# Layer 0's weights loaded in fewer transfers on two queues, and the first stripe's buffers in another place

## Chip, cores and metric

The kernel runs on one core of a Trainium2 chip. The metric is device time in microseconds (us), median over runs. The engines are TensorE (PE; its weight loads are PEld), VectorE (DVE), ScalarE (ACT), GpSimd (POOL) and SyncE (SP). SP issues DMA transfers; in the kernel before, it issues all of them.

## The reference, cut to what matters

The input `x` is (2, 96, 96, 96): two images of 96 channels, 96 x 96. Two layers follow each other, each with a mixer and a feed-forward network, both with residuals.

```
# layer 0
x = x + conv0(ln_c(x), weights)       # see below
t = tokens(x); t = t + ffn0(ln_t(t)); x = back(t)
# layer 1
x = x + conv1(ln_c(x), weights)       # attention on pooled queries, depthwise 5x5
t = tokens(x); t = t + ffn1(ln_t(t)); x = back(t)

# conv0, for each window of 6 x 6 (k: four scan directions, d: 192 channels, n: 16 states)
xin, z = split(in_proj_w @ x); z = silu(z)
t   = gelu(bn(conv3x3(xin, off1_w)))           # offsets: fr = sigmoid(2 * off2_w @ t)
xs  = bilinear(xin, fr)
x_dbl = x_proj @ xs                            # 6 rows for dt, 16 for B, 16 for C
delta = softplus(dt_projs_weight @ x_dbl[:6] + dt_projs_bias)
A   = -exp(A_logs)
h   = h * exp(delta * A) + delta * xs * B      # scan over the 36 tokens
y   = sum_n(h * C) + Ds * xs
out = out_proj @ (ln(y) * z)
```

The weights that this case is about are small: `dt_projs_weight` (4, 192, 6), `dt_projs_bias` (4, 192), `A_logs` (768, 16) and `Ds` (768). One weight is large: `off1_w` (192, 192, 3, 3), 1296 KB.

## The kernel before

`tile_metaformer` makes constants, then calls `_layer0` and `_layer1`. `_layer0` has two parts.

The first part loads and prepares weights. `_l0_weights` (from L265 on) loads, in this order and all from SP: `in_proj`, `off1`, `out_proj`, `ln_g`, `ln_b` (L272), `bn` (L289), `off2` (L301), `x_proj` (L308). Then, for each of four directions `kg`, it loads two pieces of `dt_w` (L323, L324) and six of `dt_b` (L330, L333), each 32 numbers that land one to a partition. DVE rearranges `dt_w` into `w_dt` (L340, L346). `A_logs` is rearranged through a scratch tensor `ad` in DRAM: 16 transfers write it (L381), four read it back into `at0` (L387), DVE rearranges that into `at` (L390), PE transposes it into `pa` (L392), ACT takes the exponential into `k.A` (L395). `Ds` follows (L400). DVE also builds selection matrices from the identity: `selb` (L359, 24 copies), `minus` and `fold`. `_ffn_weights` loads four arrays (L248). All temporaries of this part come from a pool `l0t`, and PSUM from a pool `l0p`; both are closed before the second part.

The second part works on 32 stripes of six image rows. `front(n)` (`_l0_front`) loads the rows of stripe n into `xt` (L464), normalises (first matmul on x: `axc`, L475), projects, convolves (`pc`, L536), samples (`top`, `bot`), and writes `delta` and `delta * x` to DRAM (`dl_d`, `du_d`). `_l0_scan` reads them back, repeated for the 16 states (`dlr`, `dur`, L983; `cre`, L993), and for 64 units a stripe does `dA` on ACT (L997), `bp` on DVE (L1011), the scan `h` on DVE (L1021), `h * C` on POOL (L1024) and the sum on PE (L1034). `back(n)` does the rest and the feed-forward network.

The order in this second part is not that of the code. `_Plan` takes each operation with an estimated cost and a due time, simulates five engines and issues the operations by that; `_in_order` then ties each engine to that order, SP included. The plan starts at zero and knows nothing of the weights. Ahead of the plan, in the weights' part, the layer that builds the program orders each engine's instructions itself. It also gives each transfer one of eight completion semaphores in turn; a transfer that takes a semaphore waits until the transfer that had it last has landed. Memory is handed out as a stack: a pool that opens takes the place of one that has closed, and its first users wait for those who used that place. In the kernel before, `front` is the first pool that opens after `l0t` closes:

```
P.front, P.hand, P.rep, P.back = (pool(n, 1) for n in ("front", "hand", "rep", "back"))
P.ps = pool("ps0", 1, space=PSUM)
```

`_layer1` loads its weights (L1692, L248, `lb` L1706) and then, image by image, stripes `nxt` of the scratch tensor `x2d` that layer 0 wrote (L1108; first matmul `nxc`, L1113).

Of the kernel before, what the change touches and what calls it, by code (L numbers as in the profile page):

```python
# [8 lines left out]
F32 = mybir.dt.float32  # L9
# [16 lines left out]
C = 96  # L26
# [7 lines left out]
NS = 16  # L34
KG = 4
NQ = 4
CB = 32
NBL = C // CB
PAST = 1e33
EXP_LN = 6  # L40
NG = 12
# [14 lines left out]
def _in_order(k, tc, start, engines=ENGINES):  # L56

    last = {}
    for i in k.nc.cur_bb.bb.instructions[start:]:
        if i.engine in engines:  # L60
            if i.engine in last:
                tc.add_manual_dep(
                    i,
                    last[i.engine].name,
                    mybir.DependencyInfo(
                        mybir.DependencyClass.NoSync, mybir.DependencyReason.DATA
                    ),
                    reason="in_order",
                )
            last[i.engine] = i  # L70
# [170 lines left out]
def _ffn_weights(k, const, tmp, pre, W1t, b1t, W2t, b2t):  # L241

    nc = k.nc
    w = Ctx()

    def quantized(src, shape, name, keep8):
        f = tmp.tile(shape, F32, tag=name, name=pre + name)
        nc.sync.dma_start(f, src)  # L248
        q = (const if keep8 else tmp).tile(shape, F8, tag=pre + name + "q", name=pre + name + "q")
        nc.vector.tensor_copy(q, f, saturate=False)  # L250
        if keep8:
            return q
        g = const.tile(shape, F32, tag=pre + name + "g", name=pre + name + "g")
        nc.vector.tensor_copy(g, q)
        return g

    w.w1 = quantized(W1t, [C, HID], "w1", True)
    w.w2 = quantized(W2t, [128, NM, C], "w2", True)
    w.b1 = quantized(b1t, [128, NM], "b1", False)
    w.b2 = quantized(b2t, [C, 1], "b2", False)  # L260
    return w
# [5 lines left out]
def _l0_weights(k, a, cp, tmp, ps, dram):  # L267
    nc = k.nc
# [45 lines left out]
    dt_w = tmp.tile([C, 2, 3, 128], F32, tag="dt_w", name="dt_w")  # L314
# [4 lines left out]
    for kg in range(KG):  # L319
        o, kk = kg % 2, kg // 2  # L320
        nc.vector.tensor_copy(k.w_dl[:, :, o, kk * 6 : kk * 6 + 6], xp[:, :, kg, 0:6])
        rows = slice(kk * 6, kk * 6 + 6)
        nc.sync.dma_start(dt_w[rows, o, kk, :], a["dt_w"][kg, :, 0:128])  # L323
        nc.sync.dma_start(dt_w[rows, o, 2, kk * 64 : kk * 64 + 64], a["dt_w"][kg, :, 128:])  # L324
        b = a["dt_b"]
        for blk in range(2 * NBL):
            half, r = divmod(blk, NBL)
            src = b[r * CB : r * CB + CB, kg, half : half + 1]
            if blk < 4:
                nc.sync.dma_start(k.dt_b[blk::4, o, kk : kk + 1], src)  # L330
            else:
                r0 = kk * 64 + blk - 4
                nc.sync.dma_start(k.dt_b[r0 : kk * 64 + 64 : 2, o, 2:3], src)  # L333
        for j in range(4):
            src = xp[:, :, kg, 6 + NS :] if j == 1 else xp[:, :, kg, 6 : 6 + NS]
            nc.vector.tensor_copy(k.w_bc[:, :, o, j, kk, :], src)

    for o in range(2):
        for m in range(2):
# [4 lines left out]
        for kk in range(2):  # L344
            cols = slice(kk * 64, kk * 64 + 64)
# [31 lines left out]

    ad = dram.tile([NS, KG * 2, C], F32, tag="ad", name="ad")
    src = a["A_logs"].rearrange("(n d) (k g) -> n d k g", n=NS, g=NG)
    for n in range(NS):  # L380
        nc.sync.dma_start(ad[n].rearrange("k (d g) -> d k g", g=NG), src[n])  # L381
    na = KG * 2 * NBL
    at0 = tmp.tile([NQ * na, NQ, CB], F32, tag="at0", name="at0")
    at = tmp.tile([NQ * na, 128], F32, tag="at", name="at")
    rows = ad.rearrange("(q i) k (b c) -> i (k b) q c", i=NQ, c=CB)
    for i in range(NQ):
        nc.sync.dma_start(  # L387
            at0[i * na : (i + 1) * na], rows[i]
        )
    nc.vector.tensor_copy(at.rearrange("p (c q) -> p q c", c=CB), at0)  # L390
# [6 lines left out]


    ds4 = tmp.tile([C, KG, 2], F32, tag="ds4", name="ds4")
    nc.sync.dma_start(ds4, a["Ds"])  # L400
    k.Dsum = cp.tile([C, 2], F32, tag="Dsum", name="Dsum")
    nc.vector.tensor_tensor(k.Dsum, ds4[:, 0], ds4[:, 1], ALU.add)
    nc.vector.tensor_tensor(k.Dsum, k.Dsum, ds4[:, 2], ALU.add)
# [532 lines left out]
def _l0_scan(k, P, S, n, f, tau):  # L936


    nc = k.nc
    f.Y = S.tile(P.hand, [C, 2, T], "Y", 1)  # L940
    for h in range(2):

        py = S.tile(P.ps, [128, 512], "y", 1)
        t0 = (64 * n + 32 * h) * tau

        def direct(h=h, py=py):

            for b in range(NBL):
                w = k.w_D[:, h, b * CB : b * CB + CB]
                v = f.xs0.ap[:, h]  # L950
                nc.tensor.matmul(py.ap[b * CB : b * CB + CB, :HEAD], w, v[:, :HEAD],
                                 start=True, stop=False)
                nc.tensor.matmul(_tail(py, b), w, v[:, HEAD:], start=b == 0, stop=False)

        S.op("pe", 1.4, direct, (f.xs0,), (py,), due=t0)
        for o in range(2):
            for kk in range(2):
                _l0_section(k, P, S, f, o, h, kk, py, t0 + (16 * o + 8 * kk) * tau, tau)

        def out(h=h, py=py):  # L960
            nc.scalar.copy(f.Y.ap[:, h, :HEAD], py.ap[:C, :HEAD])
            for b in range(NBL):
                nc.scalar.copy(f.Y.ap[b * CB : b * CB + CB, h, HEAD:], _tail(py, b))

        S.op("act", 1.4, out, (py,), (f.Y,), due=t0 + 33 * tau)
# [84 lines left out]
def _layer0(k, tc, a, x, x2d):  # L1050


    nc = k.nc
    with ExitStack() as st:
        P = Ctx()
        pool = lambda name, bufs, **kw: st.enter_context(tc.tile_pool(name=name, bufs=bufs, **kw))
        cp = pool("l0c", 1)
        P.dram = pool("scr", 1, space=DRAM)
        with ExitStack() as ws:
            tmp = ws.enter_context(tc.tile_pool(name="l0t", bufs=1))  # L1060
            wps = ws.enter_context(tc.tile_pool(name="l0p", bufs=1, space=PSUM))
            _l0_weights(k, a, cp, tmp, wps, P.dram)
            ffn = _ffn_weights(k, cp, tmp, "f0", a["W1_0"], a["b1_0"], a["W2_0"], a["b2_0"])
        P.front, P.hand, P.rep, P.back = (pool(n, 1) for n in ("front", "hand", "rep", "back"))
        P.ps = pool("ps0", 1, space=PSUM)
        P.early = {"pe": 60, "act": 60, "dve": -30, "pool": 0, "sp": 8}
        P.np, P.ng, P.nda, P.nh = 3, 5, 2, 6
        start = len(nc.cur_bb.bb.instructions)
        S, tau = _Plan(k), 3.4
        stripes = [(b, s) for b in range(NB) for s in range(NW)]  # L1070
        F = [Ctx() for _ in stripes]

        def front(n):
            if n < len(stripes):
                t0, t1 = (64 * n - 90) * tau, (64 * n - 12) * tau
                _l0_front(k, P, S, F[n], x, *stripes[n], lambda v: t0 + v * (t1 - t0))

        def back(n):
            b, s = stripes[n]
            t0, t1 = (64 * n + 68) * tau, (64 * n + 135) * tau  # L1080
            _l0_back(k, P, S, F[n], ffn, x[b, :, s * WIN : (s + 1) * WIN, :],
                     x2d[b, :, s * T : (s + 1) * T], lambda v: t0 + v * (t1 - t0))

        front(0)
        for n in range(len(stripes)):
            front(n + 1)
            _l0_scan(k, P, S, n, F[n], tau)
            back(n)
        S.issue()
        _in_order(k, tc, start, ENGINES + (mybir.EngineType.SP,))  # L1090
# [660 lines left out]
def tile_metaformer(ctx: ExitStack, tc: tile.TileContext, a, out):  # L1751
# [33 lines left out]
    scratch = ctx.enter_context(tc.tile_pool(name="x2d", bufs=1, space=DRAM))  # L1785
    x2d = scratch.tile([NB, C, NTOK], F32, tag="x2d", name="x2d")
    _layer0(k, tc, a, a["x"], x2d)
    _layer1(k, tc, a, x2d, out)

# [61 lines left out]
```

## Time and profile before

| what | us |
|---|---|
| median of 3 runs (lowest, highest) | 9014.57 (9014.46, 9014.84) |
| profiled execution: its own time | 9021.88 |
| profiled execution: span, first to last instruction | 9020.1 |
| SP's first issue | 0.75 |
| issue of the first `xt` | 44.44 |
| first matmul on x (`axc`) | 47.60 |
| first scan (`h`, L1021) | 178.82 |
| last `h * C` of layer 0 on POOL (L1024) starts | 6889.72 |
| first matmul of layer 1's stripes (`nxc`) | 6933.29 |

| engine | busy us | share of the span |
|---|---|---|
| PE | 7473.2 | 83% |
| DVE | 8098.6 | 90% |
| ACT | 6393.2 | 71% |
| POOL | 6194.7 | 69% |

A share is a mean over stages with different limits: layer 0 runs to about 6900 us, layer 1 after it. Rows of the timeline give start, length, engine, line, operation, output and input, and in brackets how long the engine was idle before and what ended it. Rows of the waits give who waited for what, the total, the number of times and the longest. A row of SP (`SPq`) is the issue of a transfer, not its data movement. "xN" is a group of N instructions, merged.

### The profile page before, as it was taken

The numbers are of one execution on the slowest core, as the hardware profiler recorded it, in microseconds if no ns is written. First come the engines' busy times: TensorE is split into PE (matmuls) and PEld (weight loads), VectorE is DVE, ScalarE is ACT, GpSimd is POOL, SyncE is SP. The second block draws the span as 40 slices with busy tenths as digits, with TensorE's granted clock in tenths as the row PEclk, the third lists the DMA queues.
The fourth block names the chain that finished last, engine by engine and source line by source line (L and its number), as shares of the span: only waits on it lengthen the run. The fifth ranks groups of instructions, "written<-read, shape, count | busy, mean of one in ns | idle before, by whom it ended". The sixth has DMA issues, their size and how long they took to land.

```text
span 9020.1 us, 122080 instructions
## 1 busy us (share of the span) xinstructions
PE 7473.2 (83%) x43537; PEld 3552.9 (39%) x43537; DVE 8098.6 (90%) x5663; ACT 6393.2 (71%) x10720; POOL 6194.7 (69%) x3931
## 2 busy tenths in 40 slices
PE   6888788888878887888788888878866999989998
PEld 3343334444434443344344444334423333543345
DVE  2999999999999999999999999999996898969988
ACT  4677777777777777777777777777754777677867
POOL 3988888888888888888888888898874000320013
PEclk9889888988888888888898989888866999999999
DMA  2444444444444444444444444444442000010000
GB/s 75 138 140 142 140 139 145 140 141 141 135 140 139 135 147 140 141 142 139 144 140 137 142 136 141 137 140 139 138 140 68 3 3 4 21 30 2 3 9 24
DMA packets 335679, 969.58 MB, mean 107 GB/s; under 512 B 50424, under 2 KB 52144, under 8 KB 334768
## 3 DMA queue, kind: packets, MB, share of 16 engines
q1 hardware_dynamic: 335056, 961.64, 33.7%
q8 instruction: 346, 5.67, 0.3%
q14 instruction: 277, 2.27, 0.1%
HBM read 788.04 MB, written 132.17 MB: 102 GB/s over the span
## 4 chain that ended last, share of the span: by engine, by line
DVE 39%; PE 14%; issue 3%; ACT 2%; POOL 1%; DVEq 1%; DMA 0%; SPq 0%; POOLq 0%; ACTq 0%
DVE h L1021 19%; DVE bp L1011 11%; DVE sums L1426 6%; PE sc L1352 4%; DVE acc L1585 3%; PE av L1413 3%; PE y L1034 1%; PE pp L1601 1%; PE pd L669 0%; PE nxc L1113 0%; POOL e L1550 0%; DVEq L1021 0%; PE pk L1125 0%; PE px L608 0%; PE pv L1157 0%
## 5 line engine op out<-in xcount | busy, mean ns | idle before, releaser
L1024 POOL TENSOR_TENSOR h<-h,cre 128x864 f32<-128x864 f32 x2048 | 4122.8, 2021 | 826.7 <-DVE h L1021 415.0
L1021 DVE TENSOR_TENSOR_SCAN h<-dA,bp 128x864 f32<-128x864 f32 x2048 | 4001.5, 1954 | 252.3 <-PE y L1034 6.4
L997 ACT ACTIVATE dA<-dlr,A 128x576 f32<-128x576 f32 x3072 | 2157.0, 765 | 1219.5 <-DVE h L1021 1127.9
L1011 DVE TENSOR_TENSOR bp<-dur,B 128x864 f32<-128x864 f32 x2048 | 2175.8, 1062 | 257.2 <-DMA dur<-du_d 45.5
L1034 PE MATMUL y<-h,fold 128*32 128x288 f32 (+2 forms) x18432 | 1877.9, 454 | 106.3 <-POOL h L1024 102.2
L1008 PE MATMUL B<-bt,selb 128*128 128x288 bf16 x2048 | 637.6, 313 | 1095.3 <-DVE bp L1011 1087.5
L536 PE MATMUL pc<-xin,off 96*96 96x288 f32 x4608 | 1325.0, 414 | 0.9 <-ACT xin L501 0.9
L1034 PEld LDWEIGHTS y<-h,fold 128*32 128x32 f32 x18432 | 766.0, 119 | 1359.0 <-issue 623.2
L1356 ACT ACTIVATE pr<-sc 128x960 f32<-128x960 f32 (+1 forms) x1080 | 955.4, 937 | 258.0 <-DVE sums L1426 146.1
L1426 DVE TENSOR_TENSOR sums<-sums,pr 128x1920 f32<-128x1920 f32 (+1 forms) x510 | 1059.2, 2077 | 60.2 <-ACT pr L1356 7.0
L536 PEld LDWEIGHTS pc<-xin,off 96*96 96x96 f32 x4608 | 708.0, 164 | 622.8 <-issue 379.9
L1507 POOL MEMSET vch<- 96x32 f32 x16 | 2.0, 125 | 1312.8 <-DVE dist L1385 1269.0
L1352 PE MATMUL sc<-qH,kH 32*128 32x480 f32 (+1 forms) x3240 | 710.2, 602 | 9.8 <-DMA q<-qH 9.8
L1352 PE MATMUL sc<-q,kH 32*128 32x480 f32 (+1 forms) x1080 | 564.3, 602 | 0.0
L1413 PE MATMUL av<-pr,vT 128*32 128x480 f32 (+1 forms) x4320 | 532.9, 564 | 3.8 <-ACT av L1430 3.5
L1585 DVE SCALAR_TENSOR_TENSOR acc<-vch,lepe_w,acc 96x1152 f32<-96x1152 f32 x304 | 489.9, 1612 | 7.6
L1008 PEld LDWEIGHTS <-selb 128*128 128x128 bf16 x2048 | 201.9, 100 | 710.5 <-issue 634.5
L1352 PEld LDWEIGHTS sc<-qH,kH 32*128 32x128 f32 x3240 | 285.0, 184 | 439.6 <-issue 304.3
L709 PE MATMUL pt<-xd,w_dt 96*128 96x288 f32 x768 | 317.5, 506 | 25.9 <-ACT zs L519 13.9
L728 POOL TENSOR_TENSOR e<-e,du 128x576 f32<-128x576 f32 x192 | 271.0, 1412 | 32.2 <-ACT du L724 32.0
L1550 POOL TENSOR_TENSOR e<-e,mask 100x384 f32<-100x384 f32 x96 | 171.5, 1808 | 175.6 <-ACT e L1548 175.3
L730 POOL TENSOR_TENSOR dl<-dl,r 128x576 f32<-128x576 f32 x192 | 270.2, 1407 | 6.2
(260 smaller groups left out, 10182.2 us busy)
## 6 DMA issues: line engine op xcount, KB each, us to landing
cre<-c_d SPq DMA_DIRECT2D x1024, 288.0 KB
dur<-du_d SPq DMA_DIRECT2D x256, 864.0 KB
dlr<-dl_d SPq DMA_DIRECT2D x256, 864.0 KB
x<-xs SPq DMA_DIRECT2D x512, 72.0 KB
du_d<-du SPq DMA_DIRECT2D x128, 288.0 KB
dl_d<-dl SPq DMA_DIRECT2D x128, 288.0 KB
du_d<-du SPq DMA_DIRECT2D x128, 144.0 KB
dl_d<-dl SPq DMA_DIRECT2D x128, 144.0 KB
```

Of the source, the lines that this page charges most:

```text
L536: pe(H2, lambda: nc.tensor.matmul(pc.ap[:C, :H2], k.w_c1[:, ih, tap, oh * C : (oh + 1) * C], xin.ap[:, ih, 3 * c + dy : 3 * c + dy + 3, dx ...
L997: S.op("act", 0.76, lambda blk=blk: nc.scalar.activation(dA.ap[:, :, blk, :], dlr.ap[:, blk, :].rearrange("p (c n) -> p c n", c=2), AF.Exp ...
L1008: S.op("pe", 0.3, lambda: nc.tensor.matmul(pB.ap[:, :H2], k.selb[:, kk, i, :], f.bc[o].ap[:, toks], start=True, stop=True), (f.bc[o],), (p ...
L1011: S.op("dve", 1.13, lambda: nc.vector.tensor_tensor(bp.ap[:, : NBL * H2].rearrange("p (b n) -> p b n", b=NBL), dur.ap[:, :, toks], pB.ap[: ...
L1021: nc.vector.tensor_tensor_scan(hv, dv, bv, 0.0, ALU.mult, ALU.add)
L1024: S.op("pool", 2.06, lambda: nc.gpsimd.tensor_tensor(ht.ap, ht.ap, cre.ap[:, toks].unsqueeze(1).to_broadcast([128, NBL, H2]), ALU.mult), ( ...
L1034: nc.tensor.matmul(dst, k.fold, v, start=False, stop=stop)
L1352: nc.tensor.matmul(two[s // 2][:, s % 2, :n], kH[rows, k0 : k0 + 128], q, start=True, stop=True)
L1356: nc.scalar.activation(pr[:, 2 * i : 2 * i + 2, :n], two[i][:, :, :n], AF.Exp, scale=HD**-0.5)
L1413: nc.tensor.matmul((main if s < HEADS else other)[s * HD : (s + 1) * HD, :n], vT[:, blk, hd, :], pr[:, s, :n], start=at == 0, stop=at == e ...
L1426: nc.vector.tensor_tensor(sums[:, :, :n], sums[:, :, :n], pr[:, :, :n], ALU.add)
L1585: S.op("dve", 1.6, lambda: nc.vector.scalar_tensor_tensor(acc.ap, src(), W.lw[:, t : t + 1], acc.ap, ALU.mult, ALU.add), (vch,), (acc,))
```

## The change

Transfers of `dt_w`, `ad`, `at0` and `Ds` are issued by ACT instead of SP. The 24 pieces of `dt_b` become one load of `b`, and PE puts the numbers in their places with four small matmuls: `take` and `take2` are columns of the identity in the right order. The 16 transfers into `ad` become eight, cut along another axis. In PSUM, a tile `beside` of three banks is taken and never used, ahead of `pb`. In `_layer0`, `rep` is the first pool to open after `l0t` closes, and `front` the last. In the kernel after, lines below this place in the file are 14 higher.

```
@@ _l0_weights
-        nc.sync.dma_start(dt_w[rows, o, kk, :], a["dt_w"][kg, :, 0:128])
-        nc.sync.dma_start(dt_w[rows, o, 2, kk * 64 : kk * 64 + 64], a["dt_w"][kg, :, 128:])
-        b = a["dt_b"]
-        for blk in range(2 * NBL):
-            half, r = divmod(blk, NBL)
-            src = b[r * CB : r * CB + CB, kg, half : half + 1]
-            if blk < 4:
-                nc.sync.dma_start(k.dt_b[blk::4, o, kk : kk + 1], src)
-            else:
-                r0 = kk * 64 + blk - 4
-                nc.sync.dma_start(k.dt_b[r0 : kk * 64 + 64 : 2, o, 2:3], src)
+        nc.scalar.dma_start(dt_w[rows, o, kk, :], a["dt_w"][kg, :, 0:128])
+        nc.scalar.dma_start(dt_w[rows, o, 2, kk * 64 : kk * 64 + 64], a["dt_w"][kg, :, 128:])
...
+    b = tmp.tile([C, KG, 2], F32, tag="b", name="b")
+    nc.scalar.dma_start(b, a["dt_b"])
+    take = tmp.tile([C, 2, 128], F32, tag="take", name="take")
+    take2 = tmp.tile([C, 64], F32, tag="take2", name="take2")
+    nc.vector.memset(take, 0.0)
+    for blk in range(2 * NBL):
+        half, r = divmod(blk, NBL)
+        cols = k.ident[:C, r * CB : r * CB + CB]
+        nc.vector.tensor_copy(take[:, half, blk::4] if blk < 4 else take2[:, blk - 4 :: 2], cols)
+
+    ps.tile([128, 3, 512], F32, tag="beside", name="beside")
+    pb = ps.tile([128, 2, KG], F32, tag="pb", name="pb")
+    for half in range(2):
+        nc.tensor.matmul(pb[:, 0], take[:, half], b[:, :, half], start=half == 0, stop=half == 1)
+    nc.vector.tensor_copy(
+        k.dt_b[:, :, 0:2].rearrange("p o k -> p k o"), pb[:, 0].rearrange("p (k o) -> p k o", o=2))
+    for kk in range(2):
+        rows = slice(kk * 64, kk * 64 + 64)
+        nc.tensor.matmul(pb[rows, 1, :2], take2, b[:, 2 * kk : 2 * kk + 2, 1], start=True, stop=True)
+    nc.vector.tensor_copy(k.dt_b[:, :, 2], pb[:, 1, :2])
...
-    for n in range(NS):
-        nc.sync.dma_start(ad[n].rearrange("k (d g) -> d k g", g=NG), src[n])
+    dst = ad.rearrange("n k (d g) -> n d k g", g=NG)
+    for d in range(8):
+        nc.scalar.dma_start(dst[:, d], src[:, d])
...
     for i in range(NQ):
-        nc.sync.dma_start(
+        nc.scalar.dma_start(
             at0[i * na : (i + 1) * na], rows[i]
         )
...
-    nc.sync.dma_start(ds4, a["Ds"])
+    nc.scalar.dma_start(ds4, a["Ds"])
@@ _layer0
-        P.front, P.hand, P.rep, P.back = (pool(n, 1) for n in ("front", "hand", "rep", "back"))
+        P.rep, P.hand, P.back, P.front = (pool(n, 1) for n in ("rep", "hand", "back", "front"))
```

## The prediction

> **What bounds the kernel now.** I read the page first: the span and the slices of part 2.
>
> ```profile
> span 9020.1 us, 122080 instructions
> DVE  2999999999999999999999999999996898969988
> ```
>
> After the first slice (225 us each) DVE is busy 90% or more in every slice up to about 6890 us, that is, all through layer 0. There the time is 2048 units of one `bp` product and one scan. Four-fifths of the first slice is no such work, so I read its timeline. First DVE, where the loop begins:
>
> ```profile
> 172.36 1.06 DVE L1011 TENSOR_TENSOR bp<-dur,B 128x864 f32<-128x864 f32 x1 [45.46 <-DMA dur<-du_d]
> 178.82 1.95 DVE L1021 TENSOR_TENSOR_SCAN h<-dA,bp 128x864 f32<-128x864 f32 x1 [5.39 <-ACT dA L997]
> 180.88 1.06 DVE L1011 TENSOR_TENSOR bp<-dur,B 128x864 f32<-128x864 f32 x1
> ```
>
> From 178.82 on DVE has no idle time worth naming (a unit takes 3.23 us: 16 scans from 191.57 to 243.30). Whatever moves this start moves the end. What leads to it is `front(0)`, one chain from the first matmul on x. The waits of PE in the first 60 us (total, times, longest) say what that waits for:
>
> ```profile
> PE pa L392 <- DVE at L390: 42.2, 1, 42.2
> PE axc L475 <- DMA xt<-in_x: 5.0, 1, 5.0
> ```
>
> And the SP queue (start, length) says why `xt` is late:
>
> ```profile
> 1.21 0.41 SPq L272 DMA_DIRECT2D off<-in_off  x1
> ...
> 9.51 0.27 SPq L324 DMA_DIRECT2D dt_w<-in_dt_w  x1
> 9.82 2.49 SPq L330 DMA_DIRECT2D dt_b<-in_dt_b  x4
> ...
> 22.79 0.48 SPq L323 DMA_DIRECT2D dt_w<-in_dt_w  x1
> ...
> 27.37 10.90 SPq L381 DMA_DIRECT2D ad<-in_A_logs  x16
> 38.31 0.46 SPq L400 DMA_DIRECT2D ds<-in_Ds  x1
> 38.88 1.58 SPq L387 DMA_DIRECT2D at<-ad  x4
> ...
> 44.44 0.31 SPq L464 DMA_DIRECT2D xt<-in_x  x1
> ```
>
> The reader is to see 66 issues in a row, mostly 0.3 to 0.7 us each, and the load of x as the 67th. `axc`, the first matmul on x, starts at 47.60, 3.16 us after the issue of `xt`.
>
> [...] 6% DMA share in 27.3 to 38.3 us agrees that the small ones cost issue, not bandwidth; ACT issues none in this trace. [...] 1.52 us from the issue of `dt_w` (22.79) to DVE's copy of it (24.31), and 1.69 for `Ds` (38.31 to 40.00). [...] `off1` has a bar of 0.41 us and was waited for until 9.51.
>
> **The change, part by part.** *Transfers.* 24 `dt_b` pieces become one; 16 of `ad` become 8; `dt_b`, `dt_w`, `ad`, `at0` and `Ds` go to ACT. SP keeps 13 issues ahead of `xt`, ACT gets 22. In the built order each transfer takes one of eight completion semaphores in turn, over both queues, and waits for the one eight before it. So ACT's seventh `dt_w` (L323, kg 3) waits for `off1`. `off1` is still second on SP; the 1024 packets of the old `ad` filled 6% of 11 us, so ACT's few hundred small packets delay it by some 0.1 us: issue at 9.6 instead of SP's 9.51. Its landing at +1.5, and that of the eighth `dt_w` (issue 10.0, +1.3 as 23.31 to 24.62): 11.1 and 11.3.
>
> *DVE.* In the built order all eight `w_dt` copies now stand ahead of the rest of DVE's set-up, so DVE stands still until 11.3, and is past them at 11.6. Queued behind are: `less_mean`, its fellow and `join` 0.39 (2.54 to 2.93); six `take` copies at 0.16 (nearest row `w_bc`, 0.17) 0.95; `join` 0.18; four `selb` at 0.175 (10 in 1.75) 0.70; two copies of `pb` 0.30, with a wait for PE's four new matmuls that the trace doesn't show, between 0 and 1.5, taken as 0.5. Sum 3.0: 14.6. Then the run that went from 10.22 to 14.42 before (`w_outb` to the last `w_bc`): 4.2, 18.8. Then 16 `selb` 2.8, `minus` and `fold` 0.43, `Dsum` 0.16, `f0w1q` 0.36: 22.55. Only now comes the copy `at`.
>
> *PE.* From the start of `at` to the end of ACT's `A` was 1.10 us (41.74 to 42.84), and in the built order `axc` still stands behind `pa` and waits for that `A`. So `axc` starts at about 23.7.
>
> *What is hidden behind this.* ACT after 10.3: six `ad` at 0.63, with short semaphore waits, to 14.2; `Ds` to 14.7; table and square root for `bn_s` 1.6 (10.36 to 11.96), 16.3; four `at0` at 0.4, 17.9; landing 1.28 after the last issue (40.46 to 41.74), 19.2. SP: `bn` waits for the eighth `dt_w` (11.3), then eight issues with waits for ACT's transfers; `xt` waits for `Ds` to land (14.2 + 1.7) and issues at about 16.5; x is there at 16.5 + 3.16 = 19.7. Both are some 3 us ahead of DVE; this cover gone, the start follows them one for one. `bn_s` at 16.3 is there before DVE wants it (about 17). Pool's two clears wait for nothing now. So what is late next is DVE's own set-up, not x.
>
> *Place.* `rep` lies on the weights' temporaries now, `front` does not. The first `cre` load waits for DVE work that is over by then: nothing. From `axc` on, each engine has the same instructions in the same order through layer 0, so 47.60 to 178.82 is kept, and the loop too. Gain here: 47.60 - 23.7 = 23.9.
>
> *The seam to layer 1.* In the built order, three loads `nxt` that SP issued early now stand behind `lb`:
>
> ```profile
> 6892.97 1.25 SPq L1108 DMA_DIRECT2D nxt<-x2d  x3
> ...
> 6930.41 0.42 SPq L1706 DMA_DIRECT2D lb<-in_lepe_b  x1
> ```
>
> The first issues at 6930.9. With 3.0 us for 216 KB (`xt`, 252 KB, 3.16) it is there at 6933.9; PE used it at 6933.29 (behind `lb` and `proj_b`). Loss 0.6, bounds 0 (it lands within 2.4) and 1.5 (the later two queue as well).
>
> Sum: 23.9 - 0.6 = 23.3. The profiled execution, span 9020.1 and own time 9021.88, should come to 8996.8 and 8998.6. It stands 7.3 us above the median of the runs, 9014.57, and none of the steps lies in that difference: 9014.57 - 23.3 = **8991.3**.
>
> **The rivals.** *ACT's queue binds.* The trace has no issue on ACT. If ACT pays twice SP's price, the nine issues after `off1` take 10.2 instead of 5.1: 19.8; `bn_s` 21.4; four `at0` 24.6; landing 25.9; `axc` 27.0; time 8994.6. At three times it is 33.7, and 9001.3. For it: all of `A` hangs on that queue. Against: SP's bars depend on the transfer's shape, nothing in them is SP's own. *x binds* (DVE quicker, or the semaphore waits shorter): `axc` at 19.7, 8987.3. Against: it needs DVE to lose 4 us of counted rows. *The start is swallowed*: some wait in layer 0 or at the seam stands at its place, and the gain is gone, 9014. Against: DVE's waits from 177 to 6893 sum to under 40 us, and none ends on anything but work that moves with the start. *Slower.* The pools' new order moves every buffer of the loop. If a unit of 3.23 us, in the loop of 2048, became 11.4 ns longer, the gain would be gone; above 20.2 ns (0.6%) the kernel is slower by over 0.2%; at 25 ns it gives 9014.57 - 23.3 + 51.2 = 9042.5. For it: all addresses move. Against: the same instruction has the same 1.95 us in buffers at different places (six for `h`, two for `dA`, `dur`). That the change doesn't free x at all would also end at 9014; the built order speaks against it: `xt` is SP's 14th issue, with one wait.
>
> **How the numbers follow.** About 0.2%, 18.0 us, is what a measurement of this kernel tells from no change: the line is 8996.5. DVE's set-up binds: 0.71, own range 8988.5 to 8994.5 (the wait for PE, 0.1 to 1 us for `off1`, the seam). ACT binds: 0.14, at twice the price or less 0.10, beyond the line 0.04. x binds: 0.06. Swallowed, in whole or by a third: 0.06. Slower: 0.03. Faster 0.87, no change 0.10, slower 0.03. The range from 8987.0 to 8997.5 leaves out about 0.12 in all, and takes in the dearer issue on ACT.
>
> **What would show it.** Right: `xt` issued near 16.5; ACT's seventh `dt_w` near 9.6; the copy `at` on DVE near 22.5, with DVE busy, not waiting, before it; `axc` near 23.7; the first scan near 154.9; `nxc` 0 to 1.5 us further behind the last `x2d` store. Wrong: ACT's issue bars above 1 us, or DVE idle before `at` with ACT still issuing (ACT binds); `axc` right behind `xt` (x binds); a unit other than 3.23 us; a gain at the first scan that the end of layer 0 doesn't show.

## The result, and the profile after

Six runs of the changed kernel have a median of 8985.09 us (8979.85 to 8988.45), six of the kernel before 9014.70 (9009.83 to 9028.03): ratio 0.9965, 95% interval [0.9952, 0.9977]. The forecast was 8991.3, with a range from 8987.0 to 8997.5: right in sign and in how the start is shortened, 6.2 us off in size, and 1.9 us outside the range. The same kernel was run again beside the experiments. Over all runs the kernel before has a median of 9015.93 (102 runs, 9006.83 to 9030.68) and the changed one 8988.07 (32 runs, 8979.85 to 9003.71); their means differ by 27.6 ± 2.1 us, where 23.3 was forecast. (A ± stands for 95%, from the spread of the timed runs alone.)

The page of the changed kernel, its span and DVE's slices:

```profile
span 8986.7 us, 122060 instructions
DVE  3999999999999999999999999999996998969988
```

Layer 0 is bounded by DVE as before; only the first slice has changed, from 2 to 3 tenths. What PE waits for in the first 60 us (total, times, longest, in us):

```profile
PE pb L343 <- DVE take L338: 13.2, 1, 13.2
...
PE pa L406 <- DVE Dsum L417: 7.6, 1, 7.6
```

The waits of before, 42.2 us for `at` and 5.0 for `xt`, are gone. PE's long waits are now for DVE: the small matmuls that spread `dt_b` until 13.20, and then `pa`. (`pa` reads `at`; the wait is put down to `Dsum`, the DVE row that ends at the same time.) The PE timeline (start, length, instruction, idle time before it and what ended it):

```profile
22.44 0.39 PE L406 MATMUL pa<-ident,at 96*128 96x96 f32 x1 [7.59 <-DVE Dsum L417]
23.23 2.85 PE L489 MATMUL axc<-xt,less_mean 96*96 96x384 f32 x4 [0.39 <-ACT A L409]
```

`axc`, the first matmul on x, starts at 23.23 instead of 47.60, and its releaser is ACT's `A`; x itself had landed at 20.54, by the records of landings in the trace. DVE's timeline says why `at` is late:

```profile
9.94 0.28 DVE L353 COPY w_dt<-dt_w 96x128 f32<-96x128 f32 x1 [7.05 <-DMA dt_w<-in_dt_w]
...
11.91 0.20 DVE L359 COPY w_dt<-dt_w 96x64 f32<-96x64 f32 x1 [0.31 <-DMA dt_w<-in_dt_w]
...
14.25 0.16 DVE L344 COPY dt_b<-pb 128x4 f32<-128x4 f32 x1 [0.66 <-PE pb L343]
...
18.73 2.60 DVE L372 CAST selb<-ident 32x128 bf16<-32x128 f32 x16
...
22.02 0.27 DVE L404 COPY at<-at 96x128 f32<-96x128 f32 x1
156.16 1.95 DVE L1035 TENSOR_TENSOR_SCAN h<-dA,bp 128x864 f32<-128x864 f32 x1 [6.27 <-ACT dA L1011]
```

DVE stands still for 7.05 us until `dt_w` lands, works nearly without a gap from 9.94, and the row `at` at 22.02 has no bracket: it waited for DVE's own work. The loop starts at 156.16 (178.82 before). Why `dt_w` is late shows when the two queues are read together. SP issues `off1` (`off<-in_off`, 1296 KB) early, and x much later:

```profile
1.21 0.41 SPq L272 DMA_DIRECT2D off<-in_off  x1
...
10.04 0.31 SPq L272 DMA_DIRECT2D out_proj<-in_out_proj  x1
...
16.82 0.31 SPq L478 DMA_DIRECT2D xt<-in_x  x1
```

ACT's queue:

```profile
1.23 1.30 ACTq L395 DMA_DIRECT2D ad<-in_A_logs  x2
2.56 0.73 ACTq L323 DMA_DIRECT2D dt_w<-in_dt_w  x1
...
4.36 0.31 ACTq L323 DMA_DIRECT2D dt_w<-in_dt_w  x1
9.52 0.27 ACTq L324 DMA_DIRECT2D dt_w<-in_dt_w  x1
9.83 0.31 ACTq L323 DMA_DIRECT2D dt_w<-in_dt_w  x1
...
10.52 3.82 ACTq L395 DMA_DIRECT2D ad<-in_A_logs  x6
...
16.62 1.60 ACTq L401 DMA_DIRECT2D at<-ad  x3
```

The first `dt_w`, 3 KB, was issued at 2.56 and landed at 9.84; DVE's copy of it starts at 9.94. The first `ad`, 6 KB, was issued at 1.23 and landed at 9.49; `off1` landed at 9.31. From 3.0 to 6.5 us the trace has no packet of ACT's queue at all, only those of `off1`, 13.8 KB each. So the small transfers behind `off1` land only when it has, and that is DVE's 7.05 us. It also holds up ACT's queue between 4.36 and 9.52: the next transfer has, in the built order, the completion semaphore of that first `ad`, and the one after it, at 9.83, that of `off1`. SP's `out_proj` stands until 10.04 for the semaphore of ACT's second `dt_w`, which landed at 10.03.

The time from milestone to milestone, from one profiled execution of each kernel as it stands (further ones of the same two kernels are among the experiments):

| us | before | after | difference |
|---|---|---|---|
| start of `axc` | 47.60 | 23.23 | −24.37 |
| `axc` to the first scan | 131.22 | 132.93 | +1.71 |
| first to last scan | 6708.8 | 6695.8 | −13.0 |
| last scan to `nxc` (seam) | 45.67 | 48.54 | +2.87 |
| `nxc` to the end | 2086.8 | 2086.2 | −0.6 |
| span | 9020.1 | 8986.7 | −33.4 |

The start gives what was forecast. The surprise is the line of the loop: 13.0 us less, with the same instructions. Most of the experiments after the first pair are about that line and about what limits the start now.

### The profile page after: what moved, and what is told of

Same layout as the page of the kernel before. It is cut to its first block, busy times and chain, and to the rows that moved or that the text cites. A ratio compares the mean times of both kernels' runs of the same rounds, so it can differ in the third digit from the quotient of the medians.

```text
span 8986.7 us, 122060 instructions
## 1 busy us (share of the span) xinstructions
PE 7462.2 (83%) x43545; PEld 3549.4 (39%) x43545; DVE 8094.7 (90%) x5672; ACT 6389.6 (71%) x10720; POOL 6191.0 (69%) x3931
## 5 line engine op out<-in xcount | busy, mean ns | idle before, releaser
L723 PE MATMUL pt<-xd,w_dt 96*128 96x288 f32 x768 | 316.5, 505 | 26.8 <-ACT zs L533 13.8
```

## The experiments

**The two halves, and both kernels again.** `place_alone` is the kernel before with the pools in the new order; `loads_alone` is the changed kernel with the pools in the old order:

```
place_alone   -P.front, P.hand, P.rep, P.back = (... "front", "hand", "rep", "back")
              +P.rep, P.hand, P.back, P.front = (... "rep", "hand", "back", "front")
loads_alone   the changed kernel with
              -P.rep, P.hand, P.back, P.front
              +P.front, P.hand, P.rep, P.back
```

`place_alone`:

> The kernel before with the pools opened in the new order (rep, hand, back, front) and all transfers as they were. Start: at and A hang on the transfers and stay at 41.7 and 42.8; the load xt no longer waits for the users of the closed pool (the last of them at about 44.2) but only for its turn on SP behind xr (42.32 + 0.42), so it issues near 42.8 instead of 44.44, and axc starts near 46.0 instead of 47.60: 1.6 us gained. Seam: the three nxt loads stand behind lb, 1.2 us lost. Theory 'clock' (the loop's extra 11 us of the first pair come from where the stretches of half TensorE clock fall, and that changes from run to run): the time is that of before within the spread, about 0 to 1 us better, and the loop, first scan to the issue of k_w, lies anywhere between 6734 and 6748. Rival 'place' (the loop itself is shorter in the new place): the loop is 6735 and the time 11 to 12 us better than before.

`loads_alone`:

> The kernel after with the pools opened in the old order (front first), all transfers as in after. Start: at near 22.0 and A near 23.1 as in after; the load xt waits for A, for w_D and the last f0 casts on DVE (about 23.2), issues near 23.6, and x is there 3.2 us later: axc near 26.9 instead of 23.23, so 20.7 us are gained against before at this point. Seam as in before, nothing lost. Theory 'clock': the median is 20 to 21 us better than before plus or minus some 4 us for the runs' spread, 2 to 3 us behind after, and the loop lies anywhere between 6734 and 6748. Rival 'place': the loop is that of before, 6746, and the kernel is 13 us behind after.

The changed kernel and the kernel before, unchanged:

> The kernel after, unchanged, a second profile and five more timed runs beside before. Theory 'clock': start as before (axc near 23.2, first scan near 156), the loop from first scan to the issue of k_w differs from the 6734.8 of the first profile by several us, with the time that DVE waits for PE in it differing by as much; the gap of the medians comes out between 22 and 31 us. Rival 'place': the loop is within 1 us of 6734.8 and the gap again 29 to 34.

> The kernel before, unchanged, a second profile. Theory 'clock': axc near 47.6, first scan near 178.8, but the loop from first scan to the issue of k_w differs from the 6746.1 of the first profile by several us, shorter as well as longer possible. Rival 'place': the loop is within 1 us of 6746.1.

The PE timeline of `place_alone`:

```profile
45.95 2.84 PE L475 MATMUL axc<-xt,less_mean 96*96 96x384 f32 x4 [3.30 <-DMA xt<-in_x]
```

and of `loads_alone`:

```profile
26.84 2.84 PE L489 MATMUL axc<-xt,less_mean 96*96 96x384 f32 x4 [3.83 <-DMA xt<-in_x]
```

With the loads alone, `axc` waits for x again. At `axc` the place is worth 47.60 − 45.95 = 1.65 us, the loads 47.60 − 26.84 = 20.76; together 22.4, and the whole change 24.4. Timed, `place_alone` has ratio 0.9998 [0.9990, 1.0006] (means −1.6 ± 3.0 us) and `loads_alone` 0.9978 [0.9970, 0.9985] (−20.5 ± 2.8). The time of each half agrees with what it gives at `axc`, but for the place alone that is less than the noise. The new addresses alone, which the rival "slower" rested on, cost nothing that can be measured to within these 3 us.

No run takes the fewer transfers and the second queue apart. By the issue bars of the profiles, `dt_b` and `ad` hold a queue for 24.2 us in the kernel before (24 and 16 transfers) and for 5.3 in the changed one (1 and 8), so the smaller number alone could account for most of the 20.8 us (an estimate); what ACT's queue adds isn't shown.

The changed kernel again had a median of 8992.30, ratio 0.9969 [0.9957, 0.9981], and a loop of 6700.3 us instead of 6695.8; the kernel before again had a loop of 6701.1 instead of 6708.8. So most of the 13 us of the table isn't the change: two executions of one kernel lie 7.7 us apart in the loop. On the average of three profiles of before and four of the changed kernel (the others come below) it is 6703.4 and 6698.6 us, a difference of 4.8. Of this, 2.0 us lie in the first stripe: its 64 units take 213.6 to 214.5 us in the three and 212.1 to 212.3 in the four, where DVE's scan waits for PE's `y` (6.4 us in `before`, 5.0 in `after`). In the profiles with further edits to the changed kernel the first stripe takes 212.1 to 213.7.

**What sets the start now.** If DVE's set-up is the bound, work taken from DVE must bring `axc` forward. `selb_on_pool` gives the 24 casts of `selb` and its clear to GpSimd. `off1_late` issues `off1` behind the first load of x, so that ACT's `dt_w` and `ad` no longer lie behind it. `both` has both edits.

```
selb_on_pool  -nc.vector.memset(k.selb, 0.0)       +nc.gpsimd.memset(k.selb, 0.0)
              -nc.vector.tensor_copy(k.selb...     +nc.gpsimd.tensor_copy(k.selb...
off1_late     -k.w_c1 = load("off1", [C, 2, 9, 2 * C])
              +k.w_c1 = cp.tile([C, 2, 9, 2 * C], F32, tag="off1", name="off1")
               nc.sync.dma_start(xt..., x...)      # of b = 0, s = 0
              +nc.sync.dma_start(k.w_c1, k.off1)
```

> The kernel after with the 24 copies into selb, and the clear ahead of them, on POOL instead of DVE; POOL has nothing else before about 37, and selb is first used after 110. If DVE's set-up sets the start, as predicted: 24 copies at 0.163 (16 in 2.60) leave DVE, 3.9 us, the f0 casts and w_D now stand ahead of at (1.3), so DVE is ready near 19.4, together with at0's landing (last issue 18.2 + 1.3 = 19.5); at near 19.6, A 1.1 later, axc near 20.9 instead of 23.23, and the first scan earlier by as much. If ACT's queue set it instead: at stays near 22 with DVE idle before it. If x set it: axc stays where it is. In the time 2.3 us, less than the runs' spread, so the profile decides.

> The kernel after with the 1296 KB of off1 issued right behind the first xt instead of second on SP (pc, its first user, starts 15 us behind axc). In the prediction everything waits for off1 through the turn of the eight semaphores: ACT's dt_w at 9.52, SP's out_proj at 10.04, DVE's w_dt at 9.94. If that is so: out_proj issues near 1.2, no dt_w waits past 7, DVE starts near 4.1 instead of 9.94, xt issues near 8.5; then at0 (ad's issues from 7 to 10, bn_s, ad, Ds, landing 1.7, four at0 at 0.4, landing 1.3: 17.2) is last, at near 17.3, axc near 18.7 instead of 23.23, with DVE idle shortly before at. If the wait for off1 was covered by something else, axc moves by less than 2 us. pc must not wait for off1: landed near 8.9 + 9 = 18, wanted near 33.

> The kernel after with both edits: off1 behind the first xt, selb on POOL. DVE has 3.9 us less to do, but the last thing before at is now at0, from ACT's queue: at near 17.2, axc near 18.5, only 0.2 better than with off1 late alone; 4.7 better than after at the start. In the time 4.7 us better than after if the loop is that of after; theory 'clock' says that the difference of two medians is good to some 4 us only.

DVE in `selb_on_pool`:

```profile
21.19 0.28 DVE L404 COPY at<-at 96x128 f32<-96x128 f32 x1 [1.60 <-DMA at<-ad]
```

ACT's queue there:

```profile
16.80 1.24 ACTq L401 DMA_DIRECT2D at<-ad  x3
```

With 4 us less to do, DVE brings `at` forward by only 0.83 us (`axc` to 22.39) and then stands waiting for the data of `at`. They are there at 21.19, 3.15 us after the end of their last issue (18.04), where I had counted 1.28. In the changed kernel itself they landed at 20.90, 2.7 us after their last issue, so DVE binds there by 22.02 − 20.90 = 1.1 us, not by the 3 us of my working. DVE was the bound, by a margin about a third as wide as thought.

ACT's queue in `off1_late`:

```profile
10.27 1.93 ACTq L395 DMA_DIRECT2D ad<-in_A_logs  x1
12.24 0.62 ACTq L414 DMA_DIRECT2D ds<-in_Ds  x1
...
18.09 1.61 ACTq L401 DMA_DIRECT2D at<-ad  x4
```

SP's queue there:

```profile
8.45 0.31 SPq L478 DMA_DIRECT2D off<-in_off  x1
```

and DVE's timeline:

```profile
18.19 0.16 DVE L416 TENSOR_TENSOR Dsum<-ds 96x2 f32<-96x2 f32 x1 [0.99 <-DMA ds<-in_Ds]
...
21.06 0.28 DVE L404 COPY at<-at 96x128 f32<-96x128 f32 x1 [1.73 <-DMA at<-ad]
```

`dt_w` waits no longer and DVE begins at 4.52 instead of 9.94. But `off1`, now issued at 8.45, delays the small transfers beside it: the last `ad`, issued by 12.20, landed at 17.99 (`off1` at 17.27) and lets `at0` be issued only at 18.09, and `Ds`, issued at 12.24, is there for DVE at 18.19, 5.95 us later. `axc` starts at 22.27 (21.40 in `both`), where 18.7 and 18.5 were expected. The wait has moved from `dt_w` to `ad`. In time: `selb_on_pool` 0.9979 [0.9969, 0.9989], `off1_late` 0.9972 [0.9962, 0.9982], `both` 0.9964 [0.9951, 0.9978]. The last two don't differ from the changed kernel run beside them (means +0.8 ± 5.0 and −5.4 ± 6.5 us). `selb_on_pool`, with `axc` 0.8 us earlier, is slower than it by 5.9 ± 5.0 us; no run shows why.

**A version made from these.** `best` issues `off1` from ACT behind the first `asq`, where no set-up transfer is left to be delayed, and casts `selb` on DVE behind the second `xn` of the first stripe:

```
-k.w_c1 = load("off1", [C, 2, 9, 2 * C])
+k.w_c1 = cp.tile([C, 2, 9, 2 * C], F32, tag="off1", name="off1")
 nc.scalar.copy(rows(xc, c), pc.ap[:C, :N4])
+if b == 0 and s == 0 and c == 0: nc.scalar.dma_start(k.w_c1, k.off1)
 dve(... xn = xc * va)
+the 24 casts of selb, behind the xn of (b, s, c) == (0, 0, 1)
```

> The kernel after with two edits: off1 is issued by ACT behind its first asq and axc copy, and DVE builds selb behind the first two xn instead of in the set-up. From the runs off1_late and both: with off1 on the move, everything small that is issued lands only at its end (Ds 5.9 us after its issue, ad up to 7). With off1 out of the way until the start is over, ad is landed near 12.5, at0 issued 12.5 to 14, landed 1.3 to 3.1 later, and DVE, without selb, is at the end of w_D near 15: at near 16, axc near 17 instead of 23.2 (x issued near 7.5, there near 11, hidden). off1 is issued near 19.7 and lands near 28.5, pc starts 15 us behind axc, near 32: no wait. If off1 was not what held ad: axc near 21 as in both. Time 6 us better than after, the spread of medians being some 4.

DVE in `best`:

```profile
14.87 0.28 DVE L404 COPY at<-at 96x128 f32<-96x128 f32 x1 [1.40 <-DMA at<-ad]
```

PE in `best`:

```profile
16.07 2.85 PE L489 MATMUL axc<-xt,less_mean 96*96 96x384 f32 x4 [0.39 <-ACT A L409]
31.08 4.29 PE L550 MATMUL pc<-xin,off 96*96 96x288 f32 x17
```

`axc` starts at 16.07, another 7.2 us earlier, and `pc`, the reader of `off1`, waits for nothing. Yet the time is 8991.53, ratio 0.9973 [0.9963, 0.9983], means −24.7 ± 2.7 us against the kernel before: not better than the changed kernel. In its profile the stretch from `nxc` to the end takes 2095.1 us; in all four kernels with `off1` moved it takes 2091.3 to 2095.4, against 2084.6 to 2088.7 in the four profiles of the changed kernel. In the profile, that is where the 7.2 us went. Why is not settled; the kernel before has up to 2093.0 there too, so it may be chance. It goes with half clock, which the next paragraphs are about: in this stretch PE was granted only half of its clock for 163.2 us in `best` and for 142.4 to 156.7 in the four profiles of the changed kernel, and over all 17 profiles the length of the stretch and its half clock have a correlation of 0.74. That isn't yet a cause.

**Why one kernel differs from run to run.** The waits of DVE inside the loop are almost all the same in two profiles of one kernel, but one kind is not. Kernel before, and the same kernel again, each from its own waits (total, times, longest):

```profile
DVE bp L1011 <- PE B L1008: 12.3, 9, 2.4
```

```profile
DVE bp L1011 <- PE B L1008: 3.7, 5, 1.0
```

Changed kernel, and the same again, run later (`after_fourth`):

```profile
DVE bp L1025 <- PE B L1022: 3.8, 6, 0.9
```

```profile
DVE bp L1025 <- PE B L1022: 8.5, 7, 2.4
```

The loops to these are 6708.8, 6701.1, 6695.8 and 6702.5 us: where this wait is 8.6 or 4.7 us longer, the loop is 7.7 or 6.7 longer. One such wait is at unit 1435. First the kernel before, PE:

```profile
4878.90 1.17 PE L917 MATMUL pp<-xr,ident 96*96 96x288 f32 x2
4879.86 2.13 PE L920 MATMUL pp<-zs,w_outb 96*96 96x288 f32 x4
4881.78 2.00 PE L920 MATMUL pp<-Y,out_proj 96*96 96x288 f32 x4
...
4885.66 0.42 PE L1008 MATMUL B<-bt,selb 128*128 128x288 bf16 x2
```

DVE there:

```profile
4885.99 1.06 DVE L1011 TENSOR_TENSOR bp<-dur,B 128x864 f32<-128x864 f32 x1 [2.13 <-PE B L1008]
```

and the 7 us before it as one window (length; busy time of PE, PEld, DVE, ACT, POOL with the number of instructions; granted PE clock; DMA share; GB/s):

```profile
4875.80:4882.80 7.00, 7.00 (x19) 3.67 (x20) 6.56 (x5) 2.50 (x4) 7.00 (x5) 0.50 0.59 172
```

The same place in the changed kernel, PE:

```profile
4849.52 0.74 PE L931 MATMUL pp<-xr,ident 96*96 96x288 f32 x2
4850.10 1.13 PE L934 MATMUL pp<-zs,w_outb 96*96 96x288 f32 x4
4851.07 1.13 PE L934 MATMUL pp<-Y,out_proj 96*96 96x288 f32 x4
...
4854.06 0.42 PE L1022 MATMUL B<-bt,selb 128*128 128x288 bf16 x2
```

DVE:

```profile
4854.69 1.06 DVE L1025 TENSOR_TENSOR bp<-dur,B 128x864 f32<-128x864 f32 x1
```

and the window:

```profile
4846.10:4853.10 7.00, 6.99 (x36) 3.80 (x38) 6.50 (x5) 3.92 (x8) 7.00 (x5) 0.76 0.54 169
```

The matmuls `pp` take 2.13 and 2.00 us instead of 1.13 each. PE is busy without a break here, and with the clock at 0.50 it comes too late with `B`: DVE waits 2.13 us. At 0.76 it comes in time; the row of `bp` has no bracket, so DVE doesn't wait at all.

The granted clock is 0.5 or 1.0 in every record, and it changes on a grid: 3.413 us, every boundary within 8 ns of it over a whole span, and the stretches of either clock are whole multiples (10.24, 13.65, 44.37 us are 3, 4 and 13 times), but for the last one, which ends behind the span. The place of the grid against the first instruction differs from run to run: its boundaries lie 2.47 us, plus whole multiples, behind it in `before` and 2.77 in `after`. Half clock follows a PE with little work: I sorted the grid's windows at full clock, in all 17 profiles and without their first 55 us, by how long PE was busy in them. Half clock followed 2830 of the 2842 windows with PE busy under 50%, 68% of those with 50 to 60%, and 4 of the 28,226 with 70% or more.

The unit of that spot returns 16 times in a loop (scans whose number leaves 27 on division by 128). In 17 profiles that makes 272 spots. Sorted by how much of the 7 us, from 5.5 before to 1.5 after that scan's start, had half clock:

| half clock in the 7 us | spots | mean time over a normal unit, us |
|---|---|---|
| under 4 us | 200 | 0.02 (at most 0.37) |
| 4 to 5.5 us | 50 | 0.60 (at most 1.07) |
| 6.6 us or more, mostly all of it | 22 | 2.09 (1.85 to 2.30) |

At this unit, whether DVE waits goes with how much of the 7 us had half clock. That the place of the grid decides this in each run is my reading; it was not shown.

The timed runs point the same way, since each has its mean granted clock on record. Among 96 runs of the kernel before, the five with 0.886 or less average 9025.4 us and the 14 with 0.891 9013.5; time and clock have a correlation of −0.49, so about a quarter of the variance goes with the clock. The slowest of the 32 runs of the changed kernel, 9003.71, had 0.840, all others 0.886 to 0.891.

**Taking the half clock away.** `warm` repeats the matmul of `B` four times more in the ten units of 64 that have little PE work, so as to keep the clock up. `best_warm` does so in `best`.

```
-lambda: nc.tensor.matmul(pB...)
+lambda: [nc.tensor.matmul(pB...) for _ in range(
+    5 if round(t0 / tau) % 64 in (0, 1, 2, 8, 9, 16, 20, 24, 30, 34) else 1)]
```

> The kernel after with the matmul B issued five times over instead of once (same operands, same result) in ten of the 64 units of a stripe, 0, 1, 2, 8, 9, 16, 20, 24, 30 and 34, the units in which PE is busy under half of the time and after which the trace shows half clock. Theory 'clock': half clock follows units with an idle PE and makes the next burst of matmuls late. With PE kept busy in these units, half clock in the loop falls from 1733 to 1830 us to below 1000, the step of unit 9 of most stripes from 4.34 to near 3.3 (some 20 times 1 us), stalls at unit 27 of every other stripe go, and the loop comes to 6670 to 6685 instead of 6695 to 6706; the time 15 to 25 us better than after. Rival 'PE load' (DVE waits for PE because PE has too much to do, the clock being beside the point): the loop becomes longer, by up to 10 x 32 x 0.6 us. Rival 'place': no change.

> Both of the last two: axc near 17 and the loop of warm. If both hold, 21 to 31 us better than after, 45 to 60 better than before.

Both missed. Half clock in the loop fell only from 1783.8 us to 1571.6, because PE runs `B` two to three units ahead and the repeats landed in other units than meant; the loop took 6698.7 us, and the times are 0.9967 [0.9955, 0.9979] and 0.9969 [0.9957, 0.9981], as without, though the mean clock of these runs rose to 0.900 to 0.904. Another long step of the loop that I had aimed at isn't a wait either. DVE's timeline in `warm`:

```profile
609.23 1.39 DVE L911 TENSOR_TENSOR Y<-Y,yva 96x576 f32<-96x576 f32 x2
```

It is DVE's own work between two scans. So the clock's effect on the loop rests on the 272 spots, on the correlation and on profiles of one kernel set side by side, not on an experiment that took it away; the one that took a part away, at other places than meant, gained nothing.

**The start alone held back.** If all of the gain is the start, the changed kernel with its start put back must be as slow as the kernel before. In `after_delayed` the copy `at` is made 81 times, which holds PE and `axc` back with no transfer and no place moved; it was run twice, the second time together with the changed kernel:

```
-nc.vector.tensor_copy(at.rearrange("p (c q) -> p q c", c=CB), at0)
+for _ in range(81): nc.vector.tensor_copy(at.rearrange("p (c q) -> p q c", c=CB), at0)
```

> The kernel after with its start held back by 24.4 us: the copy at on DVE is made 81 times over, each behind the one before (some 0.30 apart), so that A and axc come where they come in the kernel before, near 47.6. Everything else, transfers, places and orders, is that of after. Theory 'start' (the change gives its 24.4 us at axc, less 1 to 2 at the seam, and no more; the rest of the gap seen is the half clock's doing in each run): the time is that of before, 0 to 2 us behind it. Theory 'more' (some 5 us come from transfers or places elsewhere): the time is 3 to 5 us better than before.

> The same kernel again, for more timed runs and a second profile; expected as after_delayed. If axc lies off 47.6, the difference is taken off the time.

> The kernel after, unchanged, beside the delayed one in one call. Theory 'start': it is 24.4 us better than after_delayed, and 22 to 24 better than before. Theory 'more': 24.4 better than after_delayed, and 27 to 29 better than before.

The changed kernel had been run once more beside `off1_late`, and the kernel before beside `best`:

> The kernel after, unchanged, a third profile and more timed runs in one call with the other three. Theory 'clock': axc within 0.3 of 23.3, first scan within 1 of 156, the loop again elsewhere between 6695 and 6709 (first scan to last scan; 6695.8 and 6700.3 so far, 6708.8 and 6701.1 for before), the extra being stalls of 2 us or less at units whose number leaves 27 when divided by 128, in those stripes alone where PE ran the 7 us ahead at half clock. The gap to before 23 to 30 us. Rival 'place': a loop within 1 of 6696.

> The kernel before, unchanged, a third profile. Theory 'clock': axc near 47.5, first scan 178 to 179, the first stripe's 64 steps 214.5 as in the first two (212.2 in the three profiles of after), the loop 6701 to 6709, with stalls at unit 27 of some even stripes making the difference.

PE in `after_delayed`:

```profile
48.33 2.85 PE L489 MATMUL axc<-xt,less_mean 96*96 96x384 f32 x4 [0.39 <-ACT A L409]
```

`after_delayed` has ratio 0.9999 [0.9991, 1.0007] and the second 0.9997 [0.9989, 1.0005]. Over its 26 runs the mean is 9012.94, against 9015.06 for the kernel before, run beside them, (−2.1 ± 2.1 us) and 8988.02 for `after_fourth` (+24.9 ± 3.6), whose `axc` is 25.0 us earlier. The start thus carries 24.9 ± 3.6 of the 27.6. Held to the start of before, the kernel is still 2.1 ± 2.1 faster, though its `axc` (48.2 on average) is 0.5 later than that of before (47.7) and the seam loses 1.3 (below): a rest of about 4 ± 2 us has no cause shown. The time thus lies between the two theories. Neither half of the change shows it alone, but each is good to 3 us only. In the profiles the rest is in the loop (4.8 us less on average) and from `nxc` to the end (2086.5 against 2090.4, 3.9 less), both with single profiles of one kernel as far apart (up to 8.6 and 6.2). `after_third` (8990.09, 0.9973 [0.9964, 0.9982]) and `after_fourth` (8986.98, 0.9972 [0.9962, 0.9982]) repeat the changed kernel, `before_third` (9015.67) the one before.

## Why the prediction was right, and where it was off

*The start: right.* ACT's queue stood until 9.52 (9.6 forecast). The instruction held is the sixth `dt_w`, behind ACT's own `ad`, not the seventh behind `off1`: the forecast let `off1` hold up others through its semaphore and did not see that what is issued behind it lands late. The time came out all the same, since `ad` and `off1` landed 0.2 us apart. DVE was past the `w_dt` copies at about 12.1 (11.6), waited 0.66 us for PE's `pb` (0.5), and reached `at` at 22.02 (22.55) without a wait ahead of it; `axc` started at 23.23 (23.7); `xt` was issued at 16.82 (16.5), and at 16.54 to 17.09 in the other three profiles. Over three profiles of before and four of after, `axc` moved from 47.74 to 23.24 on average: 24.5 us, where 23.9 was forecast. The waits that end at `axc` rule out "x binds" and "ACT binds": ACT's bars are of the length of SP's (six `ad` in 3.82 us, 0.64 each, against sixteen in 10.90 on SP, 0.68 each; `dt_w` 0.27 to 0.73 against 0.27 to 0.48).

*The cover: mis-sized, without effect.* The landing of `at0` was counted at 1.28 us after the last issue and is 2.7, with x on the way; DVE binds by 1.1 us instead of 3. x landed at 20.54 instead of 19.7. A set-up on DVE lighter by more than 1.1 us would have made this step wrong.

*The seam: right in direction, small.* The `nxt` loads now stand behind `lb` on SP's queue:

```profile
6896.66 0.42 SPq L1720 DMA_DIRECT2D lb<-in_lepe_b  x1
6897.18 1.31 SPq L1122 DMA_DIRECT2D nxt<-x2d  x3
```

and PE waits for them:

```profile
6900.48 3.16 PE L1127 MATMUL nxc<-nxt,less_mean 96*96 96x288 f32 x6 [1.14 <-DMA nxt<-x2d]
```

The stretch from the last scan to `nxc` is 48.0 us on average against 46.7: a loss of 1.3 where 0.6 was taken, inside the bounds of 0 to 1.5.

*The step that failed* is "47.60 to 178.82 is kept, and the loop too" and, for the base, "none of the steps lies in that difference": what changes behind `axc`, the seam apart, was put at nothing. The instructions are kept; the times aren't, even in one and the same kernel. From `axc` to the first scan seven profiles of the two kernels show 126.5 to 132.9 us, the loop 6695.8 to 6708.8, layer 1 from `nxc` 2084.6 to 2093.0. I took the three runs at hand, 0.4 us apart, for the spread of the kernel, built the range from the unknowns of the start alone, and passed over the fact that the profiled execution stood 7.3 us above their median, which showed that executions do differ. A single run has a standard deviation of about 5 us (4.6 over the 102, 5.6 over the 32), so medians of six drawn from the 32 lie between 8983.1 and 8992.8 in 95%, and below the range's 8987.0 in about a third of the draws; the median of all 32, 8988.07, is inside the range. That the six runs fell outside is in part luck. The 6.2 us of the miss are 3.0 by which the six runs lay below the median of the 32, and 3.2 by which that median lies below the forecast. The latter comes, to within the rounding between means and medians, out of four terms: 0.6 more gain at the start than counted, 0.7 more loss at the seam, a base that is 1.4 higher (9014.57 for three runs, 9015.93 for 102), and the rest that stays open, 27.6 less 24.5 and plus 1.3, or 4.4. The reading that half clock makes the spread is supported by the 272 spots, by the clock of the timed runs and by one unit seen both ways; that it makes all of it was not shown, and a quarter of the variance is what goes with the clock.

*The rivals.* "Swallowed" did not come: `axc`'s 25 us arrive in the time one for one. That needn't hold for a further step, as `best` shows. "Slower" did not come: the unit is 3.24 us as before, and `place_alone`, which moves the addresses, costs nothing.

## What to carry to other kernels

The chain at the start was worth its full length here, 24.9 ± 3.6 us for 25.0, with a loop behind it that one engine bounds; it is read from the releaser of the first matmul on real data. A further 7.2 us, in `best`, did not arrive. When a wait is removed, work out what is next within the same few microseconds: small loads that land only with the large one ahead of them (the first `ad` at 9.49 us and the first `dt_w` at 9.84, `off1` at 9.31), and completion semaphores that pass such a delay on between two queues, made each single next cure here worth 1 us instead of the 2 to 5 that were expected. Before a range is set, ask how far two executions of the same kernel lie apart, and don't take three close runs for the answer.

## What the runs showed of the hardware that was not expected

GpSimd stretched DVE. In `both`, GpSimd casts `selb` while DVE is at its set-up:

```profile
3.04 7.45 POOL L372 CAST selb<-ident 32x128 bf16<-32x128 f32 x24
```

and DVE's timeline shows, in that time:

```profile
4.39 1.25 DVE L353 COPY w_dt<-dt_w 96x128 f32<-96x128 f32 x1 [2.04 <-DMA dt_w<-in_dt_w]
4.53 3.51 DVE L283 TENSOR_SCALAR w_outb<-out_proj,ln_b 96x96 f32<-96x96 f32 x2
5.81 4.75 DVE L283 TENSOR_SCALAR out_proj<-out_proj,ln_g 96x96 f32<-96x96 f32 x2
```

`off1_late` differs from `both` in `selb` alone. There the copy takes 0.28 us and the pairs of `L283` 0.45 and 0.44, instead of 1.25, 3.51 and 4.75 (rows overlap: the pair at 4.53 begins before the copy ends at 5.64). In all, the same seven DVE instructions take 1.4 us, from 4.52 to 5.88, in `off1_late` and 6.2 us, from 4.39 to 10.60, in `both`. One by one, the bars of GpSimd's 24 casts overlap except where one ends at 5.50, 7.98 and 10.49, and all seven DVE instructions end 0.06 to 0.18 us after one of these three times. The next copy, at 10.52, takes 0.26 us again. How the casts hold DVE back was not shown.

A small transfer's landing depends on what else is moving: the four pieces of `at0` were there 1.28 us after the last issue in the kernel before and 3.15 us after it in `selb_on_pool`, with 468 KB of x on the way (`xr` and `xt`). Behind `off1` it is worse: `Ds` took 5.95 us from its issue in `off1_late`, and the first `ad`, issued 0.02 us after `off1` from the other queue, 8.3 us in the changed kernel.
